# A graph-attention kernel: the last nine units of nodes started inside the loop over edges, and three smaller reorderings

## Chip, core and metric

The kernel runs on one core of one Trainium2 chip. The metric is the device time of one execution in microseconds (us); before the change it is 2341.86 us, the median of 3 runs (2341.75 to 2342.19).

## What is computed

One layer of attention on a graph with 12,500 nodes and 212,500 directed edges, 128 features, 8 heads of 16. Edges come sorted by their destination `dst`.

```
h = relu(layernorm(x));  q = h@Wq.T+bq;  k = edge_attr@Wk.T+bk;  v = h@Wv.T+bv      # by head
logits per edge: q[src].k, q[dst].k, q[src].q[dst]                                  # 3 x 8 numbers
score = (softmax(l1/4, dst) + softmax(l2/4, dst) + softmax(l3/4, dst)) * weight**lam
h2 = segment_sum(score * v[dst], dst)
out = x + leaky_relu(h2@Wo.T + bo, 0.1)
```

Since `v[dst]` is constant in a segment, the kernel sums only numerators and denominators of the three softmaxes over a node's edges and multiplies the sum of the three quotients by the node's own `v`.

## The kernel before, in words

**Preparation** makes q for all nodes, stores it in DRAM (`q_table`) and turns the edge indices. **The loop** then walks over the edges: they are cut into 5 streams of 84 blocks with 512 edges each; step g handles one block of stream s = g % 5, in round t = g // 5, so there are 420 steps. **The end** finishes the nodes that the loop did not.

One step on each engine, in the order in which the code issues it (a helper, `pin`, chains every instruction to the one before it on its engine, so the order of the code is the order on the engine, and each engine and each DMA queue takes its own in that order):

- GpSimd (POOL) gathers `q[src]` nine steps ahead (LOOK = 9) into a ring of 11 buffers `qq` (L623, L625), SyncE (SP) loads edge features six steps ahead (L617).
- TensorE (PE) makes k for step g+1 (`project`, L1076, L1078), spreads q[dst] for step g+1 with a 0/1 matrix into the one buffer `qd_ps` (`spread_q`, L1087), and transposes edge features of step g+2 (`turn`, L1068).
- ScalarE (ACT) copies `qd_ps` into `qq` (L1089), copies the transposed features (L1070), and makes the 0/1 matrix for the step five ahead (L1062, L1063).
- VectorE (DVE) forms the products (`logits`, L1097 needs `qd_ps` and `qq`, L1098 needs ACT's copy too) and reduces them to logits (L1100).

Behind that runs, once per round, a chain over the five steps s = 0 to 4, for the round before (t-1) and the one before that (t-2):

- s = 0: `turn_logits(t-1)` (PE L1113, L1122, ACT L1119, L1120) and `turn_sums(t-2)` (PE L1178, ACT L1179)
- s = 1: `scan_max(t-1)`, a running maximum on DVE (L1130, L1133)
- s = 2: `to_rows(t-2)`: PE L1191 compresses sums of edges into rows of nodes, ACT copies them (L1196); then `powers(t-1)`: four activations on ACT (L1141 to L1146), and one product on PE (L1148)
- s = 3: `scan_sums(t-1)` on DVE (L1154 needs the powers, L1158 twice)
- s = 4: `select(t-1)` on DVE (L1167), and `put_rows(t-2)`: five DMAs on SP's queue store rows into the DRAM tables `sums` (L1203)

Two rounds after the last step of edges (steps 420 to 429) let this chain run out.

**Nodes** are finished in units of 256. A `Nodes` object has two units (one has one): it loads `x` (L933, L936) and its sums (L959), normalizes on ACT (`normalize`, L970), turns sums into scores on DVE (`scores`, L976 to L981), transposes (`turn`: PE L985, ACT L987), makes v and weighs it (`project_v`: PE L990, L992, DVE L997), transposes again, makes the output (`project_o`: PE L990, L992, ACT L1007, DVE L1008, L1009) and stores it (L1015, L1017). 40 units are done inside the loop, in 20 pairs (`nodes_between`), each as soon as its sums are stored. The last nine units (`rest`, 5 objects) need sums of the last rounds, six of them sums of two streams, whose second part is loaded into `more` and added on DVE (L963). In the kernel before, the five `rest` objects load x in steps 425 to 429 and three of them normalize there (L1232 to L1236); all else of them stands after the loop (L1291 to L1304).

[...]

Of the kernel before, what the change touches and what calls it, by code (L numbers as in the profile page):

```python
# [7 lines left out]
F32 = mybir.dt.float32  # L8
BF = mybir.dt.bfloat16
I32 = mybir.dt.int32  # L10
AF = mybir.ActivationFunctionType
# [9 lines left out]
SLOPE = 0.1  # L21
# [451 lines left out]
def ordered_path(ctx: ExitStack, tc: tile.TileContext, flag, x, src, dst, edge_attr, edge_weight,  # L473
# [47 lines left out]
    def parts_of(u):  # L521

        return [s for s in range(S)
                if (s == 0 or START * s + RATE - NEAR < UN * (u + 1))
                and (s == S - 1 or UN * u < START * (s + 1) + RATE + NEAR)]
# [413 lines left out]
    class Nodes:  # L939
# [3 lines left out]
        def __init__(self, of):  # L943
            self.of = of
            self.n = 2 * len(of)

        def load_x(self):
            self.x = fin.tile([P, JN, F], F32, name="x_in", bufs=5)
            for i, u in enumerate(self.of):
                unit_in(self.x[:, 2 * i:2 * i + 2, :], u)  # L950

        def load_sums(self):
            self.ab = fin.tile([P, JN, 2 * H3], F32, name="ab", bufs=3)
            for i, u in enumerate(self.of):
                for j, t in enumerate(parts_of(u)):
                    to = self.ab
                    if j > 0:
                        to = self.more = fin.tile([P, JN, 2 * H3], F32, name="more", bufs=3)
                    pin(nc.sync.dma_start(to[:, 2 * i:2 * i + 2, :].rearrange("p k c -> p (k c)"),  # L959
                                          units(sums[t], u, 1, 2 * H3)[:, 0, :]))  # L960
                    if j > 0:
                        both = self.ab[:, 2 * i:2 * i + 2, :]
                        pin(nc.vector.tensor_add(both, both, to[:, 2 * i:2 * i + 2, :]))  # L963

        def normalize(self, lo, hi):
            if lo == 0:
                self.h = fin.tile([P, JN, F], F32, name="h", bufs=4)
            for b in range(lo, min(hi, self.n)):
                n = 2 * self.of[b // 2] + b % 2
                pin(nc.scalar.activation(self.h[:, b, :], self.x[:, b, :], AF.Relu,  # L970
                                         bias=shift[:, n:n + 1], scale=inv[:, n:n + 1]))

        def scores(self):
            n = self.n
            den, num = self.ab[:, :n, 0:H3], self.ab[:, :n, H3:]
            pin(nc.vector.tensor_scalar(den, den, 1e-30, None, op0=ALU.max))  # L976
            pin(nc.vector.reciprocal(den, den))
            pin(nc.vector.tensor_mul(num, num, den))
            score = self.score = fin.tile([P, JN, HEADS], F32, name="score")
            pin(nc.vector.tensor_add(score[:, :n], num[:, :, 0:HEADS], num[:, :, HEADS:2 * HEADS]))  # L980
            pin(nc.vector.tensor_add(score[:, :n], score[:, :n], num[:, :, 2 * HEADS:]))  # L981

        def turn(self, to):
            for b in range(self.n):
                pin(nc.tensor.transpose(to[:, b, :], self.h[:, b, :], ident))  # L985
            self.hT = fin.tile([P, JN, P], F32, name="hT")
            pin(nc.scalar.copy(self.hT[:, :self.n], to[:, :self.n]))  # L987

        def product(self, to, bias, w):
# [4 lines left out]

        def project_v(self, to):
            self.product(to, bv3, wv)
            pin(nc.vector.tensor_mul(  # L997
                self.h[:, :self.n, :].rearrange("p n (h d) -> p (n h) d", d=DIM),
                to[:, :self.n, :].rearrange("p n (h d) -> p (n h) d", d=DIM),
                self.score[:, :self.n, :].rearrange("p n h -> p (n h)")[:, :, None]  # L1000
                .to_broadcast([P, self.n * HEADS, DIM])))

        def project_o(self, to):
            n = self.n
            self.product(to, bo3, wo)
            o, y = self.h[:, :n], self.x[:, :n]
            pin(nc.scalar.copy(o, to[:, :n]))  # L1007
            pin(nc.vector.scalar_tensor_tensor(o, o, SLOPE, o, op0=ALU.mult, op1=ALU.max))  # L1008
            pin(nc.vector.tensor_add(y, o, y))  # L1009

        def store(self):
# [16 lines left out]
    with tc.tile_pool(name="work", bufs=2) as work, \  # L1028
# [53 lines left out]

        def spread_q(g):
            s, d = g % S, st[g // S]
            qd_ps = ps.tile([P, JN, F], F32, name="qd_ps")
            for j in range(JN):
                pin(nc.tensor.matmul(qd_ps[:, j, :], d["oh"][:, s, j * P:(j + 1) * P],  # L1087
                                     d["win"][:, s, :], start=(j == 0), stop=(j == JN - 1)))
            pin(nc.scalar.copy(qqs[g][:, :, 1, :], qd_ps))  # L1089
            qds[g] = qd_ps  # L1090
# [46 lines left out]
        def powers(t):  # L1137
            d = st[t]
            up = scan.tile([R, BE], F32, name="up")
            down = scan.tile([R, BE], F32, name="down")  # L1140
            pin(nc.scalar.activation(up, d["gap"], AF.Relu))  # L1141
            pin(nc.scalar.activation(down, d["gap"], AF.Relu, scale=-1.0))
            e = up
            keep = small([R, BE], "keep")
            pin(nc.scalar.activation(e, up, AF.Exp, scale=-SCALE))
            pin(nc.scalar.activation(keep, down, AF.Exp, scale=-SCALE))  # L1146
            att_ps = small([R, BE], "att_ps")
            pin(nc.tensor.matmul(att_ps, spread[:, 1, :], d["fa"], start=True, stop=True))  # L1148
            d.update(e=e, keep=keep, att=att_ps)

        def scan_sums(t):
# [59 lines left out]
        def nodes_between(t, s):  # L1211
            new, old = pairs.get(t - t % 2), pairs.get(t - t % 2 - 2)
            even = t % 2 == 0
            if new and even and s == 0:
                new.load_sums()
                new.load_x()
            if new and even and s == 2:
                new.normalize(0, 2)
                new.scores()
            if new and even and s == 3:  # L1220
                new.normalize(2, 4)
            if new and not even and s == 1:
                new.turn(small([P, JN, P], "node_ps"))
            if new and not even and s == 4:
                new.project_v(small([P, JN, F], "node_ps"))
            if old and even and s == 1:
                old.turn(small([P, JN, P], "node_ps"))
            if old and even and s == 4:
                old.project_o(small([P, JN, F], "node_ps"))
            if old and not even and s == 0:  # L1230
                old.store()
            if t == T + 1:  # L1232
                for r in rest[s:s + 1]:
                    r.load_x()
                for r in rest[max(s - 1, 0):min(s, 3)]:
                    r.normalize(0, 4)  # L1236

        products = str(mybir.EngineType.PE)
        fetch(0)
# [7 lines left out]
        for g in range(end + 2 * S):  # L1247
# [14 lines left out]
            if s == 0:  # L1262
                later(turn_logits, t - 1)
                later(turn_sums, t - 2)
            elif s == 1:
                later(scan_max, t - 1)
            elif s == 2:
                later(to_rows, t - 2)
                later(powers, t - 1)
            elif s == 3:  # L1270
                later(scan_sums, t - 1)
                if t + 2 < T:
                    fetch(t + 2)
            else:
                later(select, t - 1)
                later(put_rows, t - 2)
            behind[g + 1, 2] = pinned[products]
            nodes_between(t, s)
            if g < S:
                of = [u for u in range(NU) if g in parts_of(u)]  # L1280
                pin(nc.scalar.dma_start(
                    units(sums[g], of[0], len(of), 2 * H3),
                    blank[:, None, :].to_broadcast([P, len(of), 2 * 2 * H3])))


    with tc.tile_pool(name="fin_ps", bufs=2, space=PSUM) as fin_ps:
        def tile_for(name):
            return fin_ps.tile([P, JN, P], F32, name=name)

        assert len(rest) <= S  # L1290
        for r in range(len(rest) + 3):  # L1291
            if r < len(rest):
                rest[r].load_sums()
                if r >= 3:
                    rest[r].normalize(0, 4)
                rest[r].scores()
                rest[r].turn(tile_for("h_ps"))
            if 0 <= r - 1 < len(rest):
                rest[r - 1].project_v(tile_for("v_ps"))
            if 0 <= r - 2 < len(rest):  # L1300
                rest[r - 2].turn(tile_for("u_ps"))
            if 0 <= r - 3:
                rest[r - 3].project_o(tile_for("o_ps"))
                rest[r - 3].store()  # L1304


@with_exitstack
# [42 lines left out]
```

## Time and profile before

| what | us |
|---|---|
| median of 3 runs | 2341.86 |
| the profiled execution, its time | 2333.37 |
| its span in the trace | 2331.5 |
| DVE busy | 2150.8 (92%) |
| PE busy | 1812.6 (78%) |
| ACT busy | 1522.1 (65%) |
| POOL busy | 1658.1 (71%) |
| loop, from about | 150 |
| last reduction of logits ends (L1100) | 2263.8 |
| last instruction on DVE ends (L1009) | 2324.3 |

Times inside the trace count from the start of the span. The profiled execution is 8.5 us shorter than the median of the timed runs; sums made on the trace are compared with its own 2333.37 us, and their difference is carried over to the median. The engine that is busy nearly all the time in a stretch sets the pace of that stretch; the idle time of another costs nothing there. The share over the whole span hides the two ends, where another thing decides.

### The profile page before, as it was taken

How to read it: one execution, taken by the hardware profiler on the slowest of the kernel's cores; microseconds unless marked ns; L12 is line 12 of the kernel's file. 1: busy time of each engine (PE TensorE's matmuls, PEld its weight loads, DVE VectorE, ACT ScalarE, POOL GpSimd, SP SyncE). 2: the span in 40 equal slices, each digit the busy share in tenths (PEclk: the TensorE clock that was granted, in tenths of full speed). 3: DMA queues.
4: the chain of work that ended last, by engine and by line, in shares of the span. 5: the costliest groups of instructions: out<-in, count | busy, mean ns of one | idle time of the engine just before them, and what ended most of it. 6: DMA issues, size and time to landing. Idle time of an engine off the chain costs nothing. (4 is left out here: it accounts for less than half of the span.)

```text
span 2331.5 us, 35994 instructions
## 1 busy us (share of the span) xinstructions
PE 1812.6 (78%) x10629; PEld 1415.8 (61%) x10629; DVE 2150.8 (92%) x2263; ACT 1522.1 (65%) x2797; POOL 1658.1 (71%) x1715
## 2 busy tenths in 40 slices
PE   5327888888788888878878778888887777888775
PEld 4315666666666666666666566666666666666654
DVE  7659999999999999999999999999999999999983
ACT  5547676666766676666676676667666667667653
POOL 3547777777777777777777777777777777777740
PEclk9757777777778787787777787778687888688777
DMA  7657545555555555555555655554555554554522
GB/s 201 215 172 197 148 135 148 143 144 149 141 136 159 138 141 163 139 139 154 146 138 139 164 138 140 156 144 137 158 142 140 153 154 135 153 154 134 149 54 60
DMA packets 306681, 341.04 MB, mean 146 GB/s; under 512 B 137667, under 2 KB 225496, under 8 KB 306165
## 3 DMA queue, kind: packets, MB, share of 16 engines
q1 hardware_dynamic: 244906, 222.99, 32.5%
q0 software_dynamic: 54448, 112.96, 19.9%
q10 hardware_dynamic: 7120, 2.70, 0.4%
q8 instruction: 85, 1.39, 0.2%
q14 instruction: 122, 1.00, 0.1%
HBM read 307.79 MB, written 30.64 MB: 145 GB/s over the span
## 5 line engine op out<-in xcount | busy, mean ns | idle before, releaser
L625 POOL DMA_INDIRECT qq<-q_table,src_i x1680 | 1623.4, 966 | 548.6 <-issue 341.4
L1100 DVE TENSOR_REDUCE lT<-prod 128x96 f32<-128x1536 f32 x420 | 736.2, 1753 | 14.4
L1078 PE MATMUL k_ps<-wk,eT 128*128 128x128 f32 x3360 | 613.3, 338 | 103.6 <-ACT eT L1070 95.4
L1078 PEld LDWEIGHTS k_ps<-wk,eT 128*128 128x128 f32 x3360 | 518.9, 236 | 263.7 <-ACT eT L1070 180.9
L1089 ACT COPY qq<-qd_ps 128x512 f32<-128x512 f32 x420 | 245.4, 584 | 548.9 <-PE qd_ps L1087 432.2
L1098 DVE TENSOR_TENSOR prod<-qq,k_ps 128x1024 f32<-128x1024 f32 x420 | 509.8, 1214 | 0.5 <-PE k_ps L1078 0.5
L1087 PE MATMUL qd_ps<-win,oh 126*128 126x128 bf16 x1680 | 203.4, 257 | 213.4 <-DVE prod L1097 173.1
L1068 PE MATMUL eT_ps<-ident,ea 128*128 128x128 f32 x1680 | 342.0, 341 | 2.9 <-DVE found L901 2.9
L1097 DVE TENSOR_TENSOR prod<-qq,qd_ps 128x512 f32<-128x512 f32 x420 | 284.3, 677 | 47.4 <-ACT qq L1089 34.6
L1087 PEld LDWEIGHTS <-oh 126*128 126x128 bf16 x1680 | 159.5, 116 | 257.5 <-issue 208.4
L1062 ACT ACTIVATE relb<-relb,before 126x512 bf16<-126x512 bf16 x420 | 306.3, 729 | 7.4 <-DMA relb<-rel_d 7.4
L1070 ACT COPY eT<-eT_ps 128x512 f32<-128x512 f32 x420 | 246.9, 588 | 50.3 <-PE eT_ps L1068 48.7
L1063 ACT ACTIVATE oh<-relb 126x512 bf16<-126x512 bf16 x420 | 264.6, 630 | 13.4
L1068 PEld LDWEIGHTS eT_ps<-ident,ea 128*128 128x128 f32 x1680 | 243.0, 181 | 3.2 <-DVE found L901 3.2
L1178 PE MATMUL b_ps<-ident,sum 120*128 120x120 f32 x672 | 141.1, 342 | 94.8 <-ACT l L1120 92.3
L1076 PE MATMUL k_ps<-b,ones 3*128 3x512 bf16 x420 | 190.8, 454 | 5.0 <-DVE prod L1098 4.8
L1191 PE MATMUL w_ps<-back,sel 128*126 128x144 f32 x1344 | 186.9, 295 | 0.6 <-ACT back L1179 0.6
L1178 PEld LDWEIGHTS b_ps<-ident,sum 120*128 120x128 f32 x672 | 101.3, 215 | 138.6 <-ACT l L1120 111.4
L1191 PEld LDWEIGHTS w_ps<-back,sel 128*126 128x126 f32 x1344 | 178.4, 197 | 0.8 <-ACT back L1179 0.8
L1179 ACT COPY back<-b_ps 128x480 f32<-128x480 f32 x168 | 97.6, 581 | 47.0 <-PE b_ps L1178 47.0
L1130 DVE TENSOR_TENSOR_SCAN u<-l,u,far_ps 120x512 f32<-120x512 f32 x83 | 105.5, 1271 | 0.8 <-ACT l L1120 0.8
L1158 DVE TENSOR_TENSOR_SCAN sum<-keep,sum,up 120x512 f32<-120x512 f32 x83 | 105.9, 1276 | 0.0
(170 smaller groups left out, 1735.4 us busy)
## 6 DMA issues: line engine op xcount, KB each, us to landing
ea<-in_edge_attr_dram SPq DMA_DIRECT2D x419, 256.0 KB
relb<-rel_d SPq DMA_DIRECT2D x84, 630.0 KB
qq<-q_table,src_i POOLq DMA_INDIRECT x1680
win<-q_table SPq DMA_DIRECT2D x420, 31.5 KB
q_table<-q SPq DMA_DIRECT2D x24, 384.0 KB
fa<-fa_d SPq DMA_DIRECT2D x420, 4.0 KB
sums<-rows SPq DMA_DIRECT2D x416, 7.9 KB
q_table<-xq SPq DMA_DIRECT2D x24, 256.0 KB
```

The source lines that it names most:

```text
L625: rows = pin(nc.gpsimd.indirect_dma_start(out=qq[:, j, 0, :], out_offset=None, in_=q_table, in_offset=bass.IndirectOffsetOnAxis(ap=src_i[: ...
L1062: pin(nc.scalar.activation(d, d, AF.Abs, bias=before[:K3]))
L1063: pin(nc.scalar.activation(st[t]["oh"][:, s, :], d, AF.Relu, bias=1.0, scale=-1.0))
L1068: pin(nc.tensor.transpose(eT_ps[:, j, :], eas[g][:, j * F:(j + 1) * F], ident))
L1070: pin(nc.scalar.copy(eT, eT_ps))
L1078: pin(nc.tensor.matmul(k_ps[:, j, :], eTs[g][:, j, :], wk, start=False, stop=(j == JN - 1)))
L1087: pin(nc.tensor.matmul(qd_ps[:, j, :], d["oh"][:, s, j * P:(j + 1) * P], d["win"][:, s, :], start=(j == 0), stop=(j == JN - 1)))
L1089: pin(nc.scalar.copy(qqs[g][:, :, 1, :], qd_ps))
L1097: pin(nc.vector.tensor_mul(prod[:, :, 2, :], qqs[g][:, :, 0, :], qds[g]))
L1098: pin(nc.vector.tensor_mul(prod[:, :, 0:2, :], qqs[g], ks[g][:, :, None, :].to_broadcast([P, JN, 2, F])))
L1100: pin(nc.vector.tensor_reduce(lTs[t][:, :, s, :], prod.rearrange("p j i (h d) -> p j (i h) d", d=DIM), AX.X, ALU.add))
L1191: pin(nc.tensor.matmul(w_ps[:, i].rearrange("p s c -> p (s c)"), d["sel"][:, j, lo:lo + 3, :].rearrange("p s w -> p (s w)"), d["back"][:, ...
```

## The change

Four things are changed; all else, the number of units, rounds and steps too, stays.

1. **The rest begins earlier.** From step 411 (nine before the last step of edges, when no gather takes a `qq` buffer any more) `begin_rest` runs at the end of each step. The five objects load x, normalize and transpose h there, in `qq` buffers of the ring: loads at steps 411, 412, 414, 415, 417, `normalize` two steps after the load, `turn` three steps after it. Their product with Wv runs at steps 420 to 424, into five PSUM tiles that the loop no longer uses (two `eT_ps`, two `k_ps`, `qd_ps`) and that are held to the end.
2. **After the loop** all sums are loaded at once, then each object only makes scores, weighs v, transposes, and makes and stores the output.
3. **Half of the sums on ACT's queue.** The second parts (`more`, six DMAs) are issued on ACT's queue, the nine first parts on SP's. The additions of the two move into `scores`.
4. **Two edits of the round's work.** At s = 2 `powers(t-1)` stands before `to_rows(t-2)`, and inside `powers` the product on PE before the activations. In `project_o` ACT writes 0.1 times the product instead of a copy, and DVE takes the maximum of that and the product itself, read from PSUM.

```diff
-        def load_x(self):
-            self.x = fin.tile([P, JN, F], F32, name="x_in", bufs=5)
+        def load_x(self, to=None):
+            self.x = fin.tile([P, JN, F], F32, name="x_in", bufs=5) if to is None else to
...
+                both = slice(2 * i, 2 * i + 2)
+                of = parts_of(u)
+                pin(nc.sync.dma_start(self.ab[:, both, :], units(sums[of[0]], u, 1, 2 * H3)
+                                      [:, 0, :].rearrange("p (k c) -> p k c", k=2)))
+                if len(of) > 1:
+                    pin(nc.scalar.dma_start(more[:, both, :], units(sums[of[1]], u, 1, 2 * H3)
+                                            [:, 0, :].rearrange("p (k c) -> p k c", k=2)))
+                    self.more.append((self.ab[:, both, :], more[:, both, :]))
...
         def scores(self):
             n = self.n
+            for ab, more in self.more:
+                pin(nc.vector.tensor_add(ab, ab, more))
...
         def project_v(self, to):
             self.product(to, bv3, wv)
+            self.weigh(to)
+
+        def weigh(self, to):
             pin(nc.vector.tensor_mul(
...
-            pin(nc.scalar.copy(o, to[:, :n]))
-            pin(nc.vector.scalar_tensor_tensor(o, o, SLOPE, o, op0=ALU.mult, op1=ALU.max))
+            pin(nc.scalar.activation(o, to[:, :n], AF.Copy, scale=SLOPE))
+            pin(nc.vector.tensor_max(o, o, to[:, :n]))
             pin(nc.vector.tensor_add(y, o, y))
...
+            att_ps = small([R, BE], "att_ps")
+            pin(nc.tensor.matmul(att_ps, spread[:, 1, :], d["fa"], start=True, stop=True))
             pin(nc.scalar.activation(up, d["gap"], AF.Relu))
...
-            if t == T + 1:
-                for r in rest[s:s + 1]:
-                    r.load_x()
-                for r in rest[max(s - 1, 0):min(s, 3)]:
-                    r.normalize(0, 4)
+        starts, holds = (0, 1, 3, 4, 6), ("eT_ps", "eT_ps", "k_ps", "k_ps", "qd_ps")
+        late, turned = {}, {2: (0, 1), 5: (2, 3), 7: (4,)}
+        def spare():
+            return gath.tile([P, JN, 2, F], F32, name="qq").rearrange("p j i f -> p (j i f)")
+        def halves():
+            return spare().rearrange("p (i j f) -> i p j f", i=2, j=JN)
+        def begin_rest(at):
+            if at in turned:
+                late.update(zip(turned[at], halves()))
+            if at in (LOOK - 1, LOOK):
+                late[at - LOOK] = spare()
+            for r, (of, begin) in enumerate(zip(rest, starts)):
+                if at == begin:
+                    to, of.h = halves()
+                    of.load_x(to)
+                if at == begin + 2:
+                    of.normalize(0, 4)
+                if at == begin + 3:
+                    of.hT = late[r]
+                    of.turn(small([P, JN, P], "node_ps"))
+                if at == LOOK + r:
+                    of.held = ps.tile([P, JN, F], F32, name=holds[r], bufs=2 if r < 4 else 1)
+                    of.product(of.held, bv3, wv)
...
             elif s == 2:
+                later(powers, t - 1)
                 later(to_rows, t - 2)
-                later(powers, t - 1)
...
             nodes_between(t, s)
+            begin_rest(g - (end - LOOK))
...
-        for r in range(len(rest) + 3):
+        for r, of in enumerate(rest):
+            of.load_sums(*[late[k][:, r * JN * 2 * H3:(r + 1) * JN * 2 * H3].rearrange(
+                "p (j c) -> p j c", j=JN) for k in (-1, 0)])
+        for r in range(len(rest) + 2):
             if r < len(rest):
-                rest[r].load_sums()
-                if r >= 3:
-                    rest[r].normalize(0, 4)
                 rest[r].scores()
-                rest[r].turn(tile_for("h_ps"))
+                rest[r].weigh(rest[r].held)
             if 0 <= r - 1 < len(rest):
-                rest[r - 1].project_v(tile_for("v_ps"))
-            if 0 <= r - 2 < len(rest):
-                rest[r - 2].turn(tile_for("u_ps"))
-            if 0 <= r - 3:
-                rest[r - 3].project_o(tile_for("o_ps"))
-                rest[r - 3].store()
+                rest[r - 1].turn(small([P, JN, P], "node_ps"))
+            if 0 <= r - 2:
+                rest[r - 2].project_o(small([P, JN, F], "node_ps"))
+                rest[r - 2].store()
```

More of the change, by code (lines that the diff above doesn't have):

```diff
@@ L945, in __init__, with load_sums @@
             self.n = 2 * len(of)
-        def load_x(self):
-            self.x = fin.tile([P, JN, F], F32, name="x_in", bufs=5)
+            self.h = self.hT = None
+        def load_x(self, to=None):
+            self.x = fin.tile([P, JN, F], F32, name="x_in", bufs=5) if to is None else to
             for i, u in enumerate(self.of):
                 unit_in(self.x[:, 2 * i:2 * i + 2, :], u)
-        def load_sums(self):
-            self.ab = fin.tile([P, JN, 2 * H3], F32, name="ab", bufs=3)
+        def load_sums(self, to=None, more=None):
+            self.ab = fin.tile([P, JN, 2 * H3], F32, name="ab", bufs=3) if to is None else to
+            self.more = []
             for i, u in enumerate(self.of):
[L955 to L963, printed above, removed]
+                both = slice(2 * i, 2 * i + 2)
[6 more added lines that the diff above has]
+                    self.more.append((self.ab[:, both, :], more[:, both, :]))
         def normalize(self, lo, hi):
-            if lo == 0:
+            if lo == 0 and self.h is None:
                 self.h = fin.tile([P, JN, F], F32, name="h", bufs=4)
@@ L985, in turn @@
                 pin(nc.tensor.transpose(to[:, b, :], self.h[:, b, :], ident))
-            self.hT = fin.tile([P, JN, P], F32, name="hT")
+            if self.hT is None:
+                self.hT = fin.tile([P, JN, P], F32, name="hT")
             pin(nc.scalar.copy(self.hT[:, :self.n], to[:, :self.n]))
@@ L1084, in spread_q @@
             s, d = g % S, st[g // S]
-            qd_ps = ps.tile([P, JN, F], F32, name="qd_ps")
+            qd_ps = ps.tile([P, JN, F], F32, name="qd_ps", bufs=1)
             for j in range(JN):
@@ L1146, in powers @@
             pin(nc.scalar.activation(keep, down, AF.Exp, scale=-SCALE))
-            att_ps = small([R, BE], "att_ps")
-            pin(nc.tensor.matmul(att_ps, spread[:, 1, :], d["fa"], start=True, stop=True))
             d.update(e=e, keep=keep, att=att_ps)
@@ L1231, in nodes_between @@
                 old.store()
-            if t == T + 1:
-                for r in rest[s:s + 1]:
-                    r.load_x()
-                for r in rest[max(s - 1, 0):min(s, 3)]:
-                    r.normalize(0, 4)
+        starts, holds = (0, 1, 3, 4, 6), ("eT_ps", "eT_ps", "k_ps", "k_ps", "qd_ps")
+        assert len(rest) <= len(starts)
+        late, turned = {}, {2: (0, 1), 5: (2, 3), 7: (4,)}
[20 more added lines that the diff above has]
+                    of.product(of.held, bv3, wv)
         products = str(mybir.EngineType.PE)
@@ L1283, in ordered_path @@
                     blank[:, None, :].to_broadcast([P, len(of), 2 * 2 * H3])))
[L1286 to L1290, printed above, removed]
-        for r in range(len(rest) + 3):
+        for r, of in enumerate(rest):
+            of.load_sums(*[late[k][:, r * JN * 2 * H3:(r + 1) * JN * 2 * H3].rearrange(
+                "p (j c) -> p j c", j=JN) for k in (-1, 0)])
+        for r in range(len(rest) + 2):
             if r < len(rest):
-                rest[r].load_sums()
-                if r >= 3:
-                    rest[r].normalize(0, 4)
                 rest[r].scores()
-                rest[r].turn(tile_for("h_ps"))
+                rest[r].weigh(rest[r].held)
             if 0 <= r - 1 < len(rest):
-                rest[r - 1].project_v(tile_for("v_ps"))
-            if 0 <= r - 2 < len(rest):
-                rest[r - 2].turn(tile_for("u_ps"))
-            if 0 <= r - 3:
-                rest[r - 3].project_o(tile_for("o_ps"))
-                rest[r - 3].store()
+                rest[r - 1].turn(small([P, JN, P], "node_ps"))
+            if 0 <= r - 2:
+                rest[r - 2].project_o(small([P, JN, F], "node_ps"))
+                rest[r - 2].store()
 @with_exitstack
```

## The prediction, made blind

> **What bounds the kernel now.** I read the page's slices first, then the busy time by stretch, then what DVE waits for inside the loop, then the timeline of the end. On the page, the forty slices of DVE and of the granted TensorE clock:
>
> ```profile
> DVE  7659999999999999999999999999999999999983
> ...
> PEclk9757777777778787787777787778687888688777
> ```
>
> DVE is full in 35 of 40 slices; it is not at the start and in the last two (58 us each). By stretch (duration, then busy us of PE, PEld, DVE, ACT, POOL, then clock, DMA share, GB/s):
>
> ```profile
> 200.00:2200.00 2000.00, 1635.80 (x9642) 1279.20 (x9641) 1928.00 (x1829) 1352.55 (x2449) 1518.99 (x1579) 0.78 0.54 146
> ...
> 2240.00:2264.00 24.00, 16.04 (x107) 12.99 (x108) 23.76 (x23) 9.10 (x18) 9.65 (x11) 0.86 0.29 44
> 2264.00:2286.00 22.00, 16.41 (x74) 13.18 (x74) 8.60 (x10) 10.36 (x22) 0.31 (x1) 0.73 0.21 62
> 2286.00:2332.00 46.00, 25.74 (x112) 18.10 (x111) 17.84 (x46) 11.68 (x25) 0.00 (x0) 0.69 0.17 47
> ```
>
> To 2264 us DVE sets the pace (96 to 99%). From 2264 on no engine does: the last 67.5 us are a chain, in which DVE works 26.4 us. DVE's waits from 200 to 2240 us (total, times, longest) show what the loop could give:
>
> ```profile
> DVE prod L1097 <- ACT qq L1089: 23.2, 39, 1.7
> DVE prod L1097 <- DMA qq<-q_table,src_i: 11.5, 14, 1.2
> DVE h L1008 <- ACT h L1007: 11.2, 16, 0.8
> DVE ew L1154 <- ACT up L1145: 4.6, 11, 1.3
> ```
>
> Only the fourth belongs to the powers. Last the chain of the end, in the timeline (start, duration):
>
> ```profile
> 2268.38 3.62 PE L1191 MATMUL w_ps<-back,sel 128*126 128x144 f32 x16
> ...
> 2272.04 0.40 ACT L1196 COPY rows<-w_ps 126x288 f32<-126x288 f32 x1 [2.83 <-PE w_ps L1191]
> ...
> 2274.03 0.69 DVE L1154 TENSOR_TENSOR ew<-up,att_ps 120x512 f32<-120x512 f32 x1 [5.89 <-ACT up L1145]
> ...
> 2282.51 1.64 ACT L970 ACTIVATE h<-x_in,shift,inv 128x128 f32<-128x128 f32 x4 [3.97 <-DMA x_in<-in_x_dram]
> 2284.06 0.38 ACT L1196 COPY rows<-w_ps 126x288 f32<-126x288 f32 x1
> ...
> 2284.46 2.71 SPq L1203 DMA_DIRECT2D sums<-rows  x5
> ...
> 2292.50 0.26 DVE L963 TENSOR_TENSOR ab<-ab,more 128x96 f32<-128x96 f32 x1 [13.15 <-DMA more<-sums]
> ```
>
> Four pieces: the last rounds' scans (powers behind the copy of rows), the last rows (their product ends at 2282.3, but ACT sits in a normalize that waits for x, so the copy comes 1.76 us later), store and reload of sums (DVE idle 13.15 us), and from 2292.5 the rest, until DVE's last add ends at 2324.34: 31.8 us with 17.8 us of DVE work.
>
> **The change part by part.**
>
> **Powers first, in the loop.** ACT issues the same five instructions per round; the powers (2.2 us) no longer stand behind the product w_ps and 0.40 us of copy. Upper bound 4.6 us, the whole wait of L1154. Below nothing it doesn't go: the copy comes 2.2 us later, and its only reader, SP at s = 4, comes two steps (over 8 us) later; PE's product for the powers moves ahead of w_ps by 0.42 us. I take 4 us: the longest wait is 1.3 us, and most are shorter than what the powers gain.
>
> **The output's two edits.** ACT's copy (0.58 us) becomes an activation from PSUM; the nearest rows, L1145 and L1146, take 0.62 and 0.59. DVE's L1008 (0.69) becomes a two-operand maximum reading PSUM; L997 with such an operand takes 0.69. It still waits for ACT, so the 11.2 us stay. Bounds -1 and +1 us over 25 calls; I take 0.
>
> **Begin of the rest in steps 411 to 419.** ACT gets 18 normalizes of 0.41 and five copies (4 x 0.59 + 0.37): 10.1 us. PE gets 18 transposes: 4.5 x 0.6 to 1.06 = 2.7 to 4.8 us. SP gets nine loads of 0.45 us; they stand ahead of later stores of rows and of output, which wait for ACT and DVE far longer anyway (27.0 and 29.8 us from 2240 on), and behind a POOL memset (0.31) that follows the last gather at 2253.4. The ring's buffers were read two steps before they are taken. Cover: ACT is busy 28.9 of 40 us from 2200 and 9.1 of 24 from 2240, where the 0/1 matrices end. Step by step against DVE's next L1097, the tight places are steps 414 to 416: PE's clock is 0.50 from 2234 to 2244, a transpose of 1.06 goes ahead of `qd_ps`, and L1089 loses its 1.6 us of slack; then a transpose, the copies of the logits and a normalize follow. I find 0.5 us left over. Without cover it is at most 10.1 + 4.8 = 14.9 us. I take +0.5: the rows of slack are nearer than the worst case.
>
> **v made in steps 420 to 424.** Five products on PE: 4 x 1.47 + 0.92 = 6.8 us at full clock (rows at 2317.4 and 2321.0), 4 x 2.61 + 1.6 = 12 us at half. They stand in PE's order between the pieces of the chain. From 2267.39, when b_ps ends as before: first v product 2.6 (to 2270.0), transpose of the fifth object 0.55, that of the last pair 1.1 (2271.65). ACT's copy of that pair stands ahead of the powers, so these start at 2272.3, against 2272.33 before: here the gain of the new order is eaten up by the product. Then v 1.5, product of the powers 0.4 (2273.55), L1154 at 2274.0 as before; w_ps 2.12 (2275.7); v, v, the pair's output, v: 1.5 + 1.5 + 1.5 + 0.9 (2281.05); b_ps twice with ACT's copies (2283.15), w_ps 2.12 (2285.3). ACT is free now, since the normalizes are gone from here: rows stored from 2285.8, against 2284.46. So 1.3 us **later**.
>
> The clock decides this term, and here the Trainium skill ("TensorE: Matmul & The Clock Gate", section "Part 1: The HAM clock gate") is weighed: PE starts at half clock after idling and is released after some 3.4 us of steady work. In this trace PE works without a gap from 2263.87, yet the granted clock stays 0.50 until about 2271.4, 7.5 us. By the rule the first v product would run at full clock and the rows come 2 us earlier; I use the trace. Both say that a PE kept busy from there stays fast; if it stayed at half speed to 2294, rows would come 9 us later.
>
> **Reload of sums.** SP stores five rows (2.7 us, to 2288.5), then issues nine loads at 0.45 us; ACT issues six beside it. A lone reload lands 2.0 us after its issue (2309.94 to 2311.93), the first queued one took 4.0 (2288.51 to 2292.50), behind 106 KB of x that are gone. The first object needs SP's second and ACT's first load: issued 2289.0, landed 2291 to 2293; I take 2292.0. Of the skill's "DMA: Bandwidth & Descriptors", section "Issuing engines are not separate DMA queues", this edit has little to hope for: a second issuing engine saves only issue time. The DMA share of 0.38 to 0.52 between 2288 and 2292 says the same from another side: neither bytes nor engines bind, and 6 x 0.45 = 2.7 us of issue leave the path only where DVE waits for loads. By the rule and by the row I credit it 0.5 us.
>
> **The end proper.** Per object DVE now does sums and scores (2.0 with one addition, 2.12 with two), weigh 0.6, maximum and add 1.35: for 4.5 objects and six additions 18.4 us. PE transposes the second object before it makes the first output, and starts cold: weigh of the second ends at +5.3, transpose 1.1, output 2.6, copy 0.6: DVE waits 1.9 us until +9.8. Then DVE carries on (third scores before, fourth object, output two: +15.1; fifth object and output three: +18.7), the fourth output waits for PE (+20.9), the fifth ends at +22.0. So 2314.0 instead of 2324.34; the 7.2 us from DVE's last add to the end of the span remain.
>
> **Sum.** -4 (powers), +0.5 (steps 411 to 419), -10.3 (the end: +1.3 for the rows, -1.8 between rows and first score, -9.8 from first score to last add). Together -13.8 us: 2333.37 becomes 2319.6 in the trace, and 2341.86 becomes 2328.
>
> **Rivals.**
>
> *PE is the bound of the end, at half clock.* If PE stays at 0.50, rows come 9 us later and the outputs some 2 us later: the gain shrinks to about 3 us, 2339. For it: clock 0.50 in long stretches of the end. Against: these followed idle PE time, which is filled now.
>
> *ACT and PE don't hide the early work.* In steps 411 to 419 L1089 stands on ACT behind normalizes and behind copies that wait for PE's transposes; every object then costs DVE 1.65 + 1.06 + 0.59 us. Price 14.9 us; from 13.8 us of new idle time before DVE's last L1100 it is slower than before, 2343. Against: DVE waits on ACT only 0.6 us a time, and ACT has 11 and 15 us free there.
>
> *The powers do nothing.* The wait of L1154 goes, and L1097 waits as much longer for ACT: 4 us less, 2332. For: that row has five times as much wait. Against: those waits come at s = 1, before the edit.
>
> **Numbers.** Forecast (gain 8 to 18 us, with the powers' rival inside it): 0.62. Half clock in part (gain 5 to 8): 0.16; in full, within 0.2% (4.7 us, about what a measurement of this kernel can tell from no change): 0.11. More than 18 us (loads land early, PE warm at once): 0.06. Slower by over 0.2%: 0.05. So faster 0.84, same 0.11, slower 0.05. Range 2322 to 2338: the bounds +-2 for the loads, +-2 for the clock's phase, -1 to +4 for the steps of the loop, and the half-clock case up to its middle.
>
> **What would show it.** The wait of L1154 for ACT gone in the loop; the last L1100 ending near 2260; rows stored about 22 us after it; first score about 28 us after it; DVE's last add 22 us after the first score; clock 1.00 from about 8 us after the last L1100 until the last rows. Wrong if L1097 waits more for ACT from 2200 on, or the clock is 0.50 through the v products.

## The result, and the profile after

The changed kernel takes 2333.39 us (median of 6 runs, 2329.74 to 2336.81), the kernel before 2342.03 us in the same comparison: ratio 0.9959, 95% interval 0.9946 to 0.9972. It is 8.6 us faster; 2328 had been forecast, with a range of 2322 to 2338. The profiled execution took 2332.72 us, its span is 2330.8 us. A caution ahead of any comparison of the two traces: the profiled execution of the kernel before, 2333.37 us, was shorter than every timed run of that kernel, and the profiled one of the changed kernel is an ordinary one. So spans can't be subtracted (that would give 0.7 us); lengths of pieces can, where it is shown how far a piece varies by itself.

The slices of DVE and of the granted clock, from the page after; the second last slice of DVE, an 8 before, is full now, and the last has a 4 instead of a 3:

```profile
DVE  6659999999999999999999999999999999999994
...
PEclk8758777777787787878888778788797877887796
```

Busy time by stretch (duration, then busy us of PE, PEld, which is PE's loading of weights, DVE, ACT and POOL, then granted clock, DMA share, GB/s):

```profile
200.00:2200.00 2000.00, 1637.67 (x9619) 1263.94 (x9618) 1921.19 (x1826) 1341.67 (x2441) 1519.35 (x1576) 0.80 0.53 146
...
2240.00:2264.00 24.00, 18.60 (x118) 14.53 (x118) 22.96 (x23) 18.50 (x39) 14.37 (x16) 0.86 0.43 84
2264.00:2286.00 22.00, 16.71 (x89) 12.41 (x90) 15.21 (x15) 9.86 (x21) 0.00 (x0) 0.77 0.01 2
2286.00:2332.00 46.00, 22.68 (x112) 17.12 (x111) 20.80 (x50) 7.53 (x14) 0.00 (x0) 0.67 0.18 51
```

ACT's busy time from 2240 to 2264 has doubled (9.1 to 18.5 us). 7.0 us of it are normalizes and copies of the rest; 2.5 us are 0/1 matrices, which fall into this window because the last reduction ends 9.4 us later in this trace. In the 2000 us of the loop DVE works 7 us *less* than before, which means that it got less done in the same time. What DVE waited for from 200 to 2240 us (line numbers of the changed kernel: L1104 was L1097, L1096 was L1089, L1015 was L1008):

```profile
DVE prod L1104 <- DMA qq<-q_table,src_i: 24.6, 29, 2.3
DVE prod L1104 <- ACT qq L1096: 16.9, 25, 1.7
DVE h L1015 <- ACT h L1014: 9.6, 12, 0.8
```

The wait for the powers, 4.6 us before, is gone. In its place stand 14 us more before the first product of a step, L1104 (48.3 against 34.7, with two groups of 4.1 and 2.7 us that are not shown). And the timeline of the end, which begins here at 2273.24, where the last reduction of logits ends (2263.81 before):

```profile
2277.90 2.08 PE L996 MATMUL eT_ps<-wv,qq 128*128 128x128 f32 x8
...
2281.59 1.16 PE L996 MATMUL eT_ps<-wv,qq 128*128 128x128 f32 x8
...
2283.47 0.69 DVE L1161 TENSOR_TENSOR ew<-up,att_ps 120x512 f32<-120x512 f32 x1 [5.93 <-ACT up L1154]
...
2294.62 2.39 SPq L1210 DMA_DIRECT2D sums<-rows  x5
2296.58 3.11 ACTq L962 DMA_DIRECT2D qq<-sums  x6
2297.21 4.28 SPq L959 DMA_DIRECT2D qq<-sums  x9
2299.70 0.26 DVE L977 TENSOR_TENSOR qq<-qq 128x96 f32<-128x96 f32 x1 [8.14 <-DMA qq<-sums]
...
2322.86 0.43 DVE L1016 TENSOR_TENSOR qq<-qq 128x256 f32<-128x256 f32 x1
```

Counted from the end of the last reduction, in us ("first sums arrive" is the start of DVE's first addition):

| point | before | forecast | after |
|---|---|---|---|
| last powers begin on ACT | 8.5 | 8.5 | 8.5 |
| last rows are stored | 20.7 | 22.0 | 21.4 |
| first sums arrive at DVE | 28.7 | 28.2 | 26.5 |
| DVE's last add ends | 60.5 | 50.2 | 50.0 |

The end got 10.5 us shorter, 10.3 had been forecast. The loop (from the start of the first reduction to the end of the last) took 2091.6 us in the trace of before and 2097.8 in the trace of after; whether that is the change is the first thing to test.

### The profile page after: what moved, and what is told of

Its sections match the earlier page's. It is cut to its first block, busy times and chain, and to the rows that moved or that the text cites. A ratio compares the mean times of both kernels' runs of the same rounds, so it can differ in the third digit from the quotient of the medians.

```text
span 2330.8 us, 36027 instructions
## 1 busy us (share of the span) xinstructions
PE 1816.1 (78%) x10629; PEld 1402.4 (60%) x10629; DVE 2149.0 (92%) x2263; ACT 1515.6 (65%) x2797; POOL 1659.6 (71%) x1715
## 4 chain that ended last, share of the span: by engine, by line
DVE 26%; PE 22%; issue 17%; ACT 15%; DMA 14%; POOL 4%; SPq 1%; DVEq 0%; ACTq 0%; POOLq 0%
DMA qq<-q_table,src_i 10%; PE k_ps L1085 7%; DVE prod L1105 6%; DVE prod L1104 6%; PE eT_ps L1075 4%; DVE sum L1165 4%; POOL qq L625 4%; PE qd_ps L1094 3%; ACT eT L1077 3%; ACT relb L1069 3%; ACT oh L1070 2%; ACT l L1127 2%; PE b_ps L1185 2%; DVE sel L1174 2%; ACT qq L1096 2%
## 5 line engine op out<-in xcount | busy, mean ns | idle before, releaser
L1085 PE MATMUL k_ps<-wk,eT 128*128 128x128 f32 x3360 | 606.2, 335 | 62.2 <-ACT eT L1077 54.6
L1085 PEld LDWEIGHTS k_ps<-wk,eT 128*128 128x128 f32 x3360 | 512.4, 233 | 208.9 <-ACT eT L1077 143.5
L1096 ACT COPY qq<-qd_ps 128x512 f32<-128x512 f32 x420 | 245.5, 585 | 569.6 <-PE qd_ps L1094 411.8
L1104 DVE TENSOR_TENSOR prod<-qq,qd_ps 128x512 f32<-128x512 f32 x420 | 284.1, 676 | 61.3 <-ACT qq L1096 28.8
L1075 PE MATMUL eT_ps<-ident,ea 128*128 128x128 f32 x1680 | 333.7, 335 | 2.9 <-DVE found L901 2.9
L1075 PEld LDWEIGHTS eT_ps<-ident,ea 128*128 128x128 f32 x1680 | 236.2, 177 | 3.2 <-DVE found L901 3.2
L1198 PEld LDWEIGHTS w_ps<-back,sel 128*126 128x126 f32 x1344 | 171.2, 190 | 22.4 <-issue 14.0
```

The source lines that it names most:

```text
L1075: pin(nc.tensor.transpose(eT_ps[:, j, :], eas[g][:, j * F:(j + 1) * F], ident))
L1085: pin(nc.tensor.matmul(k_ps[:, j, :], eTs[g][:, j, :], wk, start=False, stop=(j == JN - 1)))
L1104: pin(nc.vector.tensor_mul(prod[:, :, 2, :], qqs[g][:, :, 0, :], qds[g]))
L1198: pin(nc.tensor.matmul(w_ps[:, i].rearrange("p s c -> p (s c)"), d["sel"][:, j, lo:lo + 3, :].rearrange("p s w -> p (s w)"), d["back"][:, ...
```

## The experiments

Theory A: the end is the whole gain, and the length of the loop varies from execution to execution whatever the order of the powers. Theory B: the new order lengthens the loop. Later two more were needed: theory C, POOL's issue of gathers paces the loop, and theory D, DVE does, as the prediction had it. All ratios are to the kernel before on the same chip.

**The kernel before, once more.**

> The kernel before, unchanged, run as if it were another. Theory A (the loop's time varies from execution to execution, the change has no part in that): time within 0.1% of the kernel before, and a profile whose loop (first to last reduction of logits) differs by some us from the 2091.6 us of the first profile, with DVE's waits for gathered rows anywhere between 10 and 25 us. Theory B (the new order of the loop makes DVE wait for gathered rows): these waits stay near 11.5 us and the loop near 2092 us.

Ratio 1.0002 (0.9992 to 1.0011). The second profile of the same kernel has a loop of 2097.9 us, 6.3 longer than the first, and from 200 to 2240 us longer waits of DVE under the gathers' name (17.1 us against 11.5) and for the powers (9.6 against 4.6):

```profile
DVE prod L1097 <- ACT qq L1089: 22.8, 41, 1.7
DVE prod L1097 <- DMA qq<-q_table,src_i: 17.1, 22, 2.2
DVE ew L1154 <- ACT up L1145: 9.6, 16, 1.6
```

So the 6.2 us between the loops of the two first traces need no effect of the change, since the same kernel differs by as much from itself, and the end is steady: 60.4 against 60.5 us. Timed runs of this kernel lie between 2334 and 2351 us. For the loop only several profiles, or timed runs, say anything.

**Only the powers** ahead of the copy of rows, in the kernel before.

```diff
             elif s == 2:
+                later(powers, t - 1)
                 later(to_rows, t - 2)
-                later(powers, t - 1)
```

(and the product ahead of the activations inside `powers`.)

> Only the powers ahead of the copy of rows. Theory A: DVE's wait for the powers in the loop, 4.6 us, goes to nothing; the time falls by 2 to 4 us (0.1 to 0.2%), the end after the last reduction stays near 60.5 us, or gets up to 3 us shorter, since w_ps no longer stands before the last powers. Theory B: the loop is 6 us longer than before, through waits for gathered rows, and the time rises by 2 to 6 us.

Ratio 0.9988 (0.9977 to 1.0000): 2.9 us less. The end is 57.6 us, 2.8 shorter (the last powers begin 5.3 us after the last reduction instead of 8.5), which accounts for the difference, though the interval also reaches to no difference. In the loop DVE's wait for the powers is 0, but the loop takes 2097.7 us: what L1154 no longer waits, L1097 waits longer (53 us in the whole loop, against 36 and 40 in the two profiles of before). The 2 to 6 us more of theory B don't show, nor does the gain in the loop of theory A.

**The changed kernel with the old order of the powers.**

> The changed kernel with the powers behind the copy of rows, as before. Theory A: 2 to 4 us slower than the changed kernel, so some 5 to 6 us faster than the kernel before; the end is longer than the 50.0 us of the changed kernel by some 2 us, since the last powers wait for w_ps again. Theory B: faster than the changed kernel, near 10 us faster than the kernel before, with waits for gathered rows near 11.5 us.

Ratio 0.9963 (0.9943 to 0.9983), the changed kernel's was 0.9959: no difference. The end is 49.7 us against 50.0, so neither the 2 to 4 us of theory A nor its "some 2 us" in the end show: the powers begin later, 11.6 us after the last reduction, but rows are copied no later (20.5 us against 21.0). In the changed kernel the order of the powers is worth nothing that can be measured.

**All sums on SP's queue.**

```diff
-                    pin(nc.scalar.dma_start(more[:, both, :], units(sums[of[1]], u, 1, 2 * H3)
+                    pin(nc.sync.dma_start(more[:, both, :], units(sums[of[1]], u, 1, 2 * H3)
```

> The changed kernel with all fifteen loads of sums on SP's queue. My account: the first object's second part comes third instead of first on another queue, 0.45 to 0.9 us later, and all later loads are hidden by DVE's work: 0.5 to 1 us slower than the changed kernel, the wait before the first addition 8.1 to 9 us. Rival (issue is the bound of the end): the last loads, issued 2.7 us later, hold up the later objects, 2 to 3 us slower.

The first addition waits 8.6 us instead of 8.1, the end is 50.4 us instead of 50.0. So taking 2.7 us of issue off SP is worth some 0.35 us, a little less than the 0.5 to 1 expected, and the rival's 2 to 3 us don't show. The ratio, 0.9947 (0.9934 to 0.9960), overlaps that of the changed kernel; its loop happened to be short (2094.4 us).

**The old output.**

> The changed kernel with the copy and the scaled maximum of before in the output. My account: no difference that can be seen, 0 to 1 us; DVE's group of the maximum has the same mean, 0.68 to 0.69 us, and its waits for ACT the same. Rival (an activation with a scale is slower than a copy, or a maximum from PSUM slower than one from SBUF): the means differ by 0.05 us or more, and the end by 0.5 us or more.

Ratio 0.9957 (0.9940 to 0.9974), end 50.0 us. ACT's activation takes 596 ns in the loop, the copy 582; DVE's maximum from PSUM 687 ns, the one it replaced 690. Nothing, as expected.

**The rest alone**, without the three small edits.

> The kernel before with the early begin of the rest, v in steps 420 to 424 and the reload of all sums at once, but the old order of powers, the old output and all sums on SP's queue. My account: this part is the whole gain: the end is 50 to 51 us, the time 0.3 to 0.5% below the kernel before. Rival (the small edits carry a part): the end is 52 us or more, the time within 0.3% of the kernel before.

Ratio 0.9959 (0.9946 to 0.9971), the ratio of the whole change, and an end of 50.2 us. The early begin and the reload in one piece are the gain; the other edits add nothing to it that can be measured.

**v behind the last rows.**

```diff
-                if at == LOOK + r:
+                if at == 16:
```

> The changed kernel with all five products of v in step 427, behind the last product w_ps, instead of steps 420 to 424. My account (they stand on PE in front of the last round's chain): powers start 4 us earlier, w_ps runs up to 9 us earlier at full clock, some 6 us earlier if PE, idle in between, is back at half clock; v itself (7 to 12 us on PE) falls into the 8 us in which PE waits for the sums, so the end shrinks from 50.0 us to 43 to 46. Rival (v is hidden in PE's idle time where it is, and moving it lays it on the path): the end grows by 2 to 4 us, since the first objects wait for their v.

Ratio 0.9930 (0.9911 to 0.9949). The end is 46.0 us, at the upper edge of what was expected: the last powers begin 6.1 us after the last reduction, rows are stored after 16.6 instead of 21.4, and all v runs while DVE waits for sums. Some of what is gained is lost again by w_ps of the round before, which ran at half clock (4.20 us) where it took 2.23.

**v in the gaps.**

```diff
                 if at == begin + 2:
                     of.normalize(0, 4)
-                if at == begin + 3:
+                if at == (3, 4, 6, 7, 12)[r]:
...
-                if at == LOOK + r:
+                if at == (7, 8, 8, 16, 16)[r]:
```

> The changed kernel with v of three objects made in steps 418 and 419, where PE waits for the last logits, v of the other two behind the last w_ps, and the fifth object's transpose in step 423. My account: as with all v behind w_ps the chain is freed, and nearly all of v lies in idle time of PE; the end is 43 to 45 us, and the first v product no longer starts at half clock in the chain. If the early three delay the last transposes of logits, the end starts 1 to 2 us late. Rival (v is hidden already): the end stays at 50 us.

Ratio 0.9932 (0.9916 to 0.9949), 2325.15 us; end 44.1 us, inside the expected 43 to 45. Its longest run, 2327.21 us, is shorter than the shortest of the changed kernel, 2329.74; from `v_after_rows` its time can't be told apart. From its timeline of the end (the last reduction ends at 2268.70):

```profile
2268.76 0.65 PE L1120 MATMUL l_ps<-ident,lT 128*120 128x128 f32 x4 [0.62 <-DVE lT L1107]
...
2273.76 4.21 PE L1198 MATMUL w_ps<-back,sel 128*126 128x144 f32 x16
...
2284.17 2.39 SPq L1210 DMA_DIRECT2D sums<-rows  x5
...
2289.32 0.26 DVE L977 TENSOR_TENSOR qq<-qq 128x96 f32<-128x96 f32 x1 [7.37 <-DMA qq<-sums]
```

PE comes to the last transposes from work and not from idling (0.62 us idle, 4.35 in the changed kernel), and they take 0.65 us instead of 1.11. Rows are stored 15.5 us after the last reduction, 5.9 earlier than in the changed kernel. So v between the pieces of the last rounds' chain cost some 6 us. The prediction had seen that it stands there, and took the place as given.

**Fewer gathers.** Nothing so far says why the powers' gain does not arrive in the loop. POOL's instructions in the changed kernel, from 1000 us on, suggest it:

```profile
1001.15 0.95 POOL L625 DMA_INDIRECT qq<-q_table,src_i  x1 [0.30 <-issue]
1002.40 0.94 POOL L625 DMA_INDIRECT qq<-q_table,src_i  x1 [0.30 <-DVE sum L1165]
1003.65 0.94 POOL L625 DMA_INDIRECT qq<-q_table,src_i  x1 [0.30 <-issue]
1004.90 0.94 POOL L625 DMA_INDIRECT qq<-q_table,src_i  x1 [0.30 <-issue]
```

A gather every 1.25 us, and never a longer pause: of 1618 pauses after 200 us in the trace of before none is over 0.35 us. The 0.30 us are the same whatever is named as the releaser, so they seem to belong to the gather. POOL "busy 71%" was full. In the trace of before it looks the same, and shows a longer gather too:

```profile
999.15 0.94 POOL L625 DMA_INDIRECT qq<-q_table,src_i  x1 [0.30 <-DMA qq<-q_table,src_i]
1000.40 1.49 POOL L625 DMA_INDIRECT qq<-q_table,src_i  x1 [0.30 <-ACT oh L1063]
1002.20 0.95 POOL L625 DMA_INDIRECT qq<-q_table,src_i  x1 [0.31 <-issue]
```

Some 5% of the gathers (85 of 1619) last over 1.1 us, so the mean distance is 1.27 us, 5.07 us for the four of a step. A step takes 4.98 us on average, but that average hides two stretches. In the trace of before the first 100 steps take 4.76 us each: they use up gathers issued ahead (the last gather of a step starts 35 us before DVE's first product at step 10, 11.5 us at step 100). The other 319 take 5.06 us, which is POOL's pace. Only in this second stretch can POOL set it.

```diff
             for j in range(JN):
+                if g % S == 4 and j == JN - 1:
+                    pin(nc.sync.dma_start(qq[:, j, 0, :], q_table[0:P, :]))
+                    continue
```

> The kernel before, in which every fifth step takes one of its four gathered sets of 128 rows as a plain load of the table's first 128 rows, on SP's queue (84 of the 1680 gathers; these edges get the wrong q[src]). Theory C (POOL's issue of gathers, one per 1.25 us, is the bound of the loop): POOL needs 1596 x 1.25 = 1995 us, the loop falls from 2092 to 2101 us to what DVE needs, 2016 us of work and 40 to 60 us of waits, so 2055 to 2075 us. Theory D (DVE sets the pace): the loop stays at 2090 to 2100 us.

> The same with the powers ahead of the copy of rows (again with wrong q[src] for one set of rows in every fifth step). Theory C: with POOL out of the way the powers' gain reaches the loop, which is 4 to 10 us shorter than with the old order, and DVE's waits for gathered rows don't grow. Rival (the powers gain nothing, whatever the bound): the loop is as long as with the old order, within 2 us.

With the old order: ratio 0.9987 (0.9970 to 1.0004), loop 2097.7 us, as without the edit. With the new order: 0.9908 (0.9890 to 0.9925), loop 2080.2 us, where `powers_only` took 2097.7. POOL now pauses, here in the old order:

```profile
1009.82 0.94 POOL L628 DMA_INDIRECT qq<-q_table,src_i  x1 [1.57 <-PE b_ps L1181]
```

Its gathers start over 40 us ahead at step 400, in both runs. So theory C holds for the new order (17.5 us go when POOL has 84 gathers less), but not in its size (2055 to 2075 us), and not for the old order: there a second limit stands at the same height. DVE's waits from 200 to 2240 us say where. With the old order two of the largest are

```profile
DVE prod L1100 <- ACT qq L1092: 31.6, 46, 1.7
DVE ew L1157 <- ACT up L1148: 9.3, 17, 1.5
```

and with the new order the second is gone, without a longer first:

```profile
DVE prod L1100 <- ACT qq L1092: 27.5, 40, 1.7
```

In the whole loop, for the powers, the first product of a step and the output: 9.3 + 38.9 + 11.6 us with the old order, 0 + 34.8 + 8.3 with the new one, 16.7 us less. So the second limit is taken to be a cycle of PE, ACT and DVE with the powers in it; the new order shortens it by some 17 us, and in the kernel with all gathers POOL's pace hides that. Each loop here is one profile, but the timed medians, 2340.5 and 2321.9 us, say the same: 15.9 us are left once 2.7 us for the shorter end are taken off, and no run of the new order (2321.1 to 2323.8) is as long as one of the old (2331.5 to 2350.3).

**Less work for DVE.**

```diff
+            some = DIM // 2 if s == S - 1 else DIM
             pin(nc.vector.tensor_reduce(lTs[t][:, :, s, :],
-                                        prod.rearrange("p j i (h d) -> p j (i h) d", d=DIM), AX.X,
+                                        prod.rearrange("p j i (h d) -> p j (i h) d", d=DIM)
+                                        [:, :, :, :some], AX.X,
```

> The kernel before, in which every fifth step reduces only 8 of the 16 products of a head (84 of 420 reductions half as long, about 0.8 us less each; these logits are wrong). Theory C: 68 us less work on DVE come back as waits, the loop gets at most 10 us shorter. Theory D: the loop gets some 60 to 68 us shorter.

Ratio 1.0011 (0.9998 to 1.0024), loop 2106.1 us: the 65 us of work taken away come back as waits (gaps on DVE in the loop 154 us, 80 in the second profile of before). POOL alone can't explain that: in the first 60 steps, at whose end gathers still start 18 us ahead, DVE works 264.5 us where it worked 273.3 in the trace of before, and they take 281.5 us against 281.9. Theory D, the prediction's "To 2264 us DVE sets the pace", is wrong, and so is the rule stated ahead of it that an engine busy nearly all the time sets the pace: DVE is busy for 96% of the loop, and less work for it makes the loop no shorter.

## Why the prediction was right, and where not

**The end was right in mechanism, and in sum partly by luck**: -10.5 us against -10.3, and a change with the rest alone has the ratio of the whole. Its terms were off in both directions and cancel. Rows came 0.7 us later, not 1.3. From rows to first sums it was 3.0 us less, not 1.8: the reload landed 2.5 us after SP's first issue, nearer to the lone reload (2.0) than to the queued one (4.0). From first sums to the last add it was 8.2 us less, not 9.8: PE fell back to half clock for the fourth output (its product took 2.08 us from 2318.27, the one before it 1.60 from 2315.00), where the forecast had it warm, and DVE waited 2.3 us for it.

**The clock at the begin of the end** came as in the trace before. PE works again from 2273.30, 7.4 of the next 7.9 us; the granted clock is 0.50 from there to 2281.20 and 1.00 from 2282 to 2294, and a v product takes 2.08 us at 2277.90 and 1.16 at 2281.59. That is some 8 us to full clock. The rule that the prediction weighed, release after some 3.4 us of steady work (the Trainium skill, "TensorE: Matmul & The Clock Gate", section "Part 1: The HAM clock gate"), would have had the first v product fast; the prediction used the trace instead, and that was right. Once fast, the chain stayed so until the last rows, as forecast; the rival of half clock to the end is out.

**Steps 411 to 419 cost nothing**: from the end of the reduction of step 410 to that of step 419 it is 46.64 us before and 46.65 after (+0.5 forecast; the second trace of before has 47.61). The queue of ACT for sums (0.35 us, 0.5 forecast) and the output (0) came about as forecast. That a second issuing engine saves only issue time (the Trainium skill, "DMA: Bandwidth & Descriptors", section "Issuing engines are not separate DMA queues") agrees with this: 2.7 us of issue were moved, and 0.35 us gained.

**The step that failed is "powers first, in the loop: I take 4 us".** The wait did go, from 2.8 to 9.6 us in four profiles with the old order to 0 in each of six with the new one, and nothing came of it: loops 2094.4 to 2098.2 us with the new order, 2091.6 to 2100.8 with the old. The third rival, "the powers do nothing", was the right one, with another reason than it had: not ACT, but POOL, whose gathers pace most of the loop. The prediction showed POOL's 1519 us of 2000 and gave it no part in the bound; it took DVE's waits as what the loop could give, and while POOL set the pace the wait that went came back before L1097. Nor was "upper bound 4.6 us, the whole wait of L1154" a bound: with fewer gathers the same order is worth 17.5 us. Its own sign for this step, the last reduction near 2260 us, did not come (2273.24). The timed gain of 8.6 us (5.2 less than the sum) fits an end of 10.5 and a loop that gives nothing; what is left, 2 us, is inside the interval of 6 us. The forecast of 2328 was 5 us off, and the time lies in its range because the range was made wide enough for this rival.

**Still open**: which of PE, ACT and DVE closes the second cycle with the old order, and why it stands so near to POOL's pace. Some 90% of the waits before L1097 in the trace of before come right after products at half clock (a spread of q in over 0.5 us instead of 0.39), but no run here held the clock. No run lengthened or shortened a single gather, so what makes one take 1.25 us is not shown.

One reading of the prediction and of the table above needs care. A wait "for DMA" before L1104 is often not one. From the trace after:

```profile
2206.39 0.63 PE L1094 MATMUL qd_ps<-win,oh 126*128 126x128 bf16 x4
...
2207.06 0.59 ACT L1096 COPY qq<-qd_ps 128x512 f32<-128x512 f32 x1 [2.41 <-PE qd_ps L1094]
...
2207.68 0.69 DVE L1104 TENSOR_TENSOR prod<-qq,qd_ps 128x512 f32<-128x512 f32 x1 [0.86 <-DMA qq<-q_table,src_i]
```

DVE starts 0.03 us after ACT's copy ends (2207.65), which had waited for PE at half clock. Of the 29 waits under that name in this loop 21 end so; in `powers_only` it is 11 of 20. The others are the gathers', and in these two traces none of them comes before step 127, when the gathers issued ahead are used up.

## What to carry to other kernels

An engine's busy share is no measure of its room: multiply the count of its instructions by their mean distance from start to start, compare that with the stretch, and see whether it ever pauses. Work issued ahead can hide such a bound for a while, so compare by stretch. Where two cycles are equally long, taking a wait out of one shows nothing until the other is shortened too, so a null result there says nothing against the edit. And work moved off the end has to be put where its engine idles: ahead of a dependency chain on the same in-order queue it lengthens that chain (5.9 us here), even when it is "early".

## What was not expected of the hardware

Issued back to back, gathers of 128 rows start 1.25 us apart on POOL (median), of which the profile shows 0.94 as busy, in all traces. Equal executions of one program differ by more than 10 us of 2340 (2334 to 2351 for the kernel before), and between its two profiles 6.3 of 6.8 us lie in the loop; the gathers after 200 us span 2051.3 us in one and 2056.9 in the other, with the same number of them.
